# Moving Mamba's and layer 2's weight loads into layer 0, and splitting the starts of layers 1, 2 and 3, in a four-layer conv-attention-Mamba kernel

## The chip, the cores and the metric

The kernel runs on one core of a Trainium2 chip. The engines of a core work side by side, each in the order of its own queue, and wait for one another on semaphores: TensorE (PE in the profile; its weight loads are PEld), VectorE (DVE), ScalarE (ACT), GpSimd (POOL) and SyncE (SP, which here only issues DMA transfers). The metric is the device time of one execution in microseconds (us); lower is better.

## What is computed

The input `x` holds 4 images of 56 x 56 tokens with 128 channels, in float32. Four layers follow one another, each with a residual; constants: 3136 tokens an image, 56 rows.

```
# layer 0: neighbourhood attention, 7 x 7 window, 4 heads, relative bias
x = x + _L0_conv_ref(_gn(x), w_qkv, b_qkv, rpb, w_proj, b_proj)
# layer 1: two Mamba blocks over each row of 56 tokens
x = x + _L1_conv_ref(_gn(x), in_proj_w, conv_w, conv_b, x_proj_w, ...)
t = _to_tokens(x)
# layer 2: additive attention over all earlier tokens, then experts choose 8 tokens each
t = t + _L2_attn_ref(_ln_t(t), W1, b1, w2, b2)
t = t + _L2_ffn_ref(_ln_t(t), gate_w, gate_b, weight1, weight2)
# layer 3: attention over all tokens, then 2 of 8 experts a token
t = t + _L3_attn_ref(_ln_t(t))
t = t + _L3_ffn_ref(_ln_t(t), router_w, router_b, expert_w, expert_b)
```

`_gn` is a group norm over an image (32 groups of 4 channels; mean and variance over all tokens); `_ln_t` a layer norm of each token. A Mamba block multiplies by `in_proj_w`, applies a causal convolution of 4 taps and a silu, makes from that the step `delta` and the vectors B and C, runs `h = exp(delta * A) * h + delta * u * B` along the row, multiplies by C and by a second silu, and projects out. The additive attention of layer 2 scores a pair of tokens by `tanh(f_i + g_j + b1) . w2`.

## The kernel before

All four images stay in SBUF, as `X[b]` of 112 partitions x 28 tiles x 128 channels. A chunk is 4 tiles, 448 tokens, 8 rows; there are 7 an image. The order of PE, ACT, DVE and POOL in each layer is written by hand (`manual_schedule`): what is emitted first stands first in an engine's queue. SP's queue, and instructions outside those regions, are ordered by the framework's scheduler, which may take a transfer that is ready ahead of one that waits. Tiles of a pool are reused; a tile of one buffer (`bufs=1`) is written again only when its readers are done.

**Group norm** (`group_norm_steps`, line 167). For each chunk: four transposes into a PSUM tile (L179), statistics on DVE (`bn_stats`, L190), a copy into the transposed image `xn` on ACT (L191). Then the statistics are aggregated, two small matmuls average over a group (L199), the root is taken on ACT (L213) and polished on DVE, and DVE norms the seven chunks in place (`normed`, L226).

**Layer 0.** `bias_tables` (line 249) reads the constant `toep` in one transfer; `make` forms 7 matmuls (L272) and 7 exponentials (L276) into `tab`, stores that whole into a DRAM table `dtab` (L279) and reads 56 slices of it back into `e_inner` and `e_edge` (L285, L295). On TensorE these matmuls stand ahead of image 0's norm. A unit is one group of key tiles for a chunk: scores (L440), exponentials (L450), multiplication by the tables (L455), weighted sums (L470); `finish` divides (L490) and projects (L496). While image b is worked on, `norm_steps(b + 1)` puts the next image's norm between its units; image 3 has no successor.

**Layer 1.** `layer1_weights` (line 550) issues 20 transfers and forms on DVE the folded weights `in_w` (L604), `A_pick` (L607), `D_diag` (L613) and `xw`; it is called at the layer's start, its pool is opened there. Then image 0's group norm runs to its end (`prepare_image(0)`), and the loop begins. `order` lists 56 blocks (image, chunk, Mamba block) of 16 pairs each. A pair is: decays (L671) and spread inputs (L680) on PE, an exponential on ACT (L696), a product (L701) and a scan (L708) on DVE, a product on POOL (L713). `mamba_pre` spreads the preparation of the next block over the pairs before: the convolution (L826), silu (L838), three projections (L844, L855, L880). All its PSUM passes go through one tile (`m`, pool `l1_m`, one buffer). Steps of a pair are kept in `first` and `last`; the loop starts at pair -18, so that block 0 has its preparation before the first scan. For images 1 to 3 the norm's steps lie among the pairs of the image before. At the end come the last gates (L734, L735), a projection (L752) and the sum into X (L768).

**Layer 2.** `layer2_attention` loads its small weights (W1, b1, w2, place, later, back; 21 transfers), forms `wf` and `wg`, calls `experts2_weights` (11 transfers and a transpose), and then runs `prepare_image(0)` to its end: statistics of 28 tiles (L977, L978), root (L149), 28 norms (L985), 7 transposed chunks (L162), the key part `g` (8 matmuls, L1001) and the queries of the first block (L1027). A block is 7 query tiles (4 blocks an image). Its pieces are `(block, key tile J, quarter q)`: sums on DVE (`adds`, L1042), tangents on ACT (L1051), scores on PE (L1062), then exponentials and weighted sums (L1073, L1076, L1089). With each piece one step is taken from the list `now` or, failing that, from others.

**Layer 3.** `table()` (L1543) asks ScalarE to load the set of tables that has both logarithm and exponential. It is called first, and again after each gelu. `normed_chunk` takes statistics (L1675), a root as `exp(-0.5 ln v)` (L1681, L1682), a Newton step (L1659 to L1662), norms (L1690) and transposes (L1701); image 0's seven chunks run before the first scores (L1597).

Of the kernel before, what the change touches and what calls it, by code (L numbers as in the profile page):

```python
# [2 lines left out]

# [15 lines left out]
S = HW * HW  # L19
# [85 lines left out]
class Hybrid:  # L105
# [37 lines left out]
    def rstd(self, pool, var, shape, eps, tag):  # L143

        nc = self.nc
        ve = self.t(pool, shape, tag + "_ve")
        nc.vector.tensor_scalar(ve, var, eps, None, op0=ALU.add)
        r = self.t(pool, shape, tag + "_r")
        nc.scalar.activation(r, ve, AF.Sqrt)  # L149
        nc.vector.reciprocal(r, r)  # L150
        q = self.t(pool, shape, tag + "_q")
        nc.vector.tensor_mul(q, r, r)
        nc.vector.tensor_mul(q, q, ve)
        nc.vector.tensor_scalar(q, q, -0.5, 1.5, op0=ALU.mult, op1=ALU.add)
        nc.vector.tensor_mul(r, r, q)
        return r
# [10 lines left out]
    def group_norm_steps(self, b, pool, psum, group, pad=0):  # L167


# [3 lines left out]
        got = {}  # L173
        chunk = lambda c: got["xn"][:, c * SEQ : (c + 1) * SEQ, pad:]

        def transposed(c):
            got["ps"] = ps = psum()
            for k in range(TC):
                nc.tensor.transpose(  # L179
                    ps[:, k * TP : (k + 1) * TP], self.X[b][:, TC * c + k, :], self.ident[:TP, :TP]  # L180
                )

        def taken(c):
            if c == 0:
                got["xn"] = self.t(pool, [P, HW, pad + HW], "xnT")
                got["st"] = self.t(pool, [P, NCH, nc.vector.BN_STATS_DIM], "gn_st")
                if pad:
                    nc.gpsimd.memset(got["xn"][:, :, 0:pad], 0.0)
            ps = got["ps"]
            nc.vector.bn_stats(got["st"][:, c, :], ps[:, :CH])  # L190
            nc.scalar.copy(chunk(c), ps[:, :CH].rearrange("p (s t) -> p s t", t=HW))  # L191

        def aggregate():
            got["mv"] = self.t(pool, [P, 2], "gn_mv")
            nc.vector.bn_aggr(got["mv"], got["st"])

        def by_group(of):
            got["ps"] = psum()
            nc.tensor.matmul(got["ps"][:, 0:1], group, of(), start=True, stop=True)  # L199

        def mean():
            got["mean"] = mean = self.t(pool, [P, 1], "gn_mean")
            nc.vector.tensor_copy(mean, got["ps"][:, 0:1])
            got["dev"] = dev = self.t(pool, [P, 1], "gn_dev")
            nc.vector.tensor_sub(dev, got["mv"][:, 0:1], mean)
            nc.vector.tensor_mul(dev, dev, dev)
            nc.vector.tensor_add(dev, dev, got["mv"][:, 1:2])

        def var():
            got["ve"] = ve = self.t(pool, [P, 1], "gn_ve")  # L210
            nc.vector.tensor_scalar(ve, got["ps"][:, 0:1], 1e-5, None, op0=ALU.add)
            got["r"] = self.t(pool, [P, 1], "gn_r")
            nc.scalar.activation(got["r"], ve, AF.Sqrt)  # L213

        def root():
            r, ve = got["r"], got["ve"]
            q = self.t(pool, [P, 1], "gn_q")
            nc.vector.reciprocal(r, r)
            nc.vector.tensor_mul(q, r, r)
            nc.vector.tensor_mul(q, q, ve)  # L220
            nc.vector.tensor_scalar(q, q, -0.5, 1.5, op0=ALU.mult, op1=ALU.add)
            nc.vector.tensor_mul(r, r, q)

        def normed(cs):
            for c in cs:
                nc.vector.tensor_scalar(  # L226
                    chunk(c), chunk(c), got["mean"], got["r"], op0=ALU.subtract, op1=ALU.mult
                )

        bind = lambda f, c: lambda: f(c)  # L230
        return got, (
            [(bind(transposed, c), bind(taken, c)) for c in range(NCH)],
            [
                aggregate, lambda: by_group(lambda: got["mv"][:, 0:1]), mean,
                lambda: by_group(lambda: got["dev"]), var, root,
            ],
            [bind(normed, cs) for cs in (range(0, 2), range(2, 4), range(4, NCH))],
        )

    def group_norm_coarse(self, *args):  # L240

        got, (chunks, stats, norms) = self.group_norm_steps(*args)
        both = lambda fs: lambda: [f() for f in fs]
        return got, [both(fs) for fs in chunks] + [both(stats[:3]), both(stats[3:])] + norms
# [4 lines left out]
    def bias_tables(self, pool, tmp, dr, m):  # L249
# [9 lines left out]
        toep = self.load(tmp, [1 + KR, S], "toep", a["k_toep"])  # L259
# [8 lines left out]
        def make():  # L268
            tab = self.t(tmp, [NH * KR, S], "tab")
            for c in range(NCH):  # L270
                ps = m()[: NH * KR]
                nc.tensor.matmul(  # L272
                    ps[:, :CH], rT.rearrange("p h r -> p (h r)"), toep[:, c * CH : (c + 1) * CH],
                    start=True, stop=True,
                )
                nc.scalar.activation(tab[:, c * CH : (c + 1) * CH], ps[:, :CH], AF.Exp)  # L276

            dtab = dr.tile([NH, KR, HW, HW], F32, name="dtab")
            nc.sync.dma_start(out=dtab.rearrange("h r k j -> (h r) (k j)"), in_=tab)  # L279
# [70 lines left out]
    def layer0(self):  # L350
# [5 lines left out]
        with ExitStack() as ctx:  # L356
# [20 lines left out]
            bproj = self.load(wp, [TP, C], "bproj", a["L0_conv_b_proj"].partition_broadcast(TP))  # L377
            for b in range(1, B):
                self.load_image(b)
            ones = self.t(wp, [TP, HD], "ones")  # L380
# [7 lines left out]
            def norm_steps(b):  # L388
                got, steps = self.group_norm_coarse(b, big, m, group)

                def hand_over():
                    steps[-1]()
                    xn[b] = got["xn"].rearrange("p i j -> p (i j)")

                return steps[:-1] + [hand_over]
# [125 lines left out]
            for k, (b, c) in enumerate(chunks):  # L521
# [9 lines left out]
                if c == 0 and b + 1 < B:  # L531
                    for n, step in enumerate(norm_steps(b + 1)):
                        add(i + 3 * n // 2, step)
            scores(0)
# [15 lines left out]
    def layer1_weights(self, wp):  # L550
        nc, a = self.nc, self.a
        w = {}
# [32 lines left out]
        with ExitStack() as ctx:  # L585
            tmp = ctx.enter_context(self.tc.tile_pool(name="l1_tmp", bufs=1))
            iw = self.load(tmp, [P, NL, DI], "iw", in_w[:, :, 0:DI])
            cw = self.t(tmp, [P, NL, DI, DC], "cw")
            nc.sync.dma_start(
                out=cw.rearrange("p l f k -> p (l f k)"),  # L590
                in_=a["L1_conv_conv_w"].rearrange("l f o k -> (l f o k)").partition_broadcast(P),
            )
            A = self.load(
                tmp, [P, NL, NHALF, DS], "A", by_channel("L1_conv_A_log", "l (h p) n -> p l h n")
            )
            nc.scalar.activation(A, A, AF.Exp)
            xw = self.load(
                tmp, [P, NL, NHALF, DBL], "xw_in", by_channel("L1_conv_x_proj_w", "l (h p) k -> p l h k")
            )
            for at, n, src in ((0, DR, 0), (HD, DR, 0), (2 * HD, DS, DR), (3 * HD, DS, DR + DS)):  # L600
                nc.vector.tensor_copy(w["xw"][:, :, :, at : at + n], xw[:, :, :, src : src + n])
            for l in range(NL):
                for k in range(DC):
# [1221 lines left out]
```

## Time and profile before

| | us |
|---|---|
| median of 3 runs (7923.6 to 7932.92) | 7929.46 |
| the profiled execution | 7930.36 |
| its span, first to last instruction | 7928.6 |
| TensorE busy in the span | 6709.2 (85%) |
| VectorE busy | 6087.8 (77%) |
| ScalarE busy | 5017.8 (63%) |
| GpSimd busy | 2551.3 (32%) |
| mean granted TensorE clock, share of full speed | 0.947 |

The rest of the profile is read stage by stage: each layer has another busiest engine, so the shares over the whole span say little. Three views matter here: the chain of waits (what ended last, followed back), the busy time of each engine in a stretch, and the order of instructions in time. All starts are in us from the start of the span. Three boundaries can be seen in the chain: about 560 (layer 0 to 1), 3544 (1 to 2) and 6407 (2 to 3).

### The profile page before, as it was taken

How to read it: one execution, taken by the hardware profiler on the slowest of the kernel's cores; microseconds unless marked ns; L12 is line 12 of the kernel's file. 1: busy time of each engine (PE TensorE's matmuls, PEld its weight loads, DVE VectorE, ACT ScalarE, POOL GpSimd, SP SyncE). 2: the span in 40 equal slices, each digit the busy share in tenths (PEclk: the TensorE clock that was granted, in tenths of full speed). 3: DMA queues.
4: the chain of work that ended last, by engine and by line, in shares of the span. 5: the costliest groups of instructions: out<-in, count | busy, mean ns of one | idle time of the engine just before them, and what ended most of it. 6: DMA issues, size and time to landing. Idle time of an engine off the chain costs nothing.

```text
span 7928.6 us, 105809 instructions
## 1 busy us (share of the span) xinstructions
PE 6709.2 (85%) x41037; PEld 2666.4 (34%) x41037; DVE 6087.8 (77%) x10253; ACT 5017.8 (63%) x4916; POOL 2551.3 (32%) x1909
## 2 busy tenths in 40 slices
PE   8878988998899899977777777777777889999999
PEld 4442333333333333322222222222222344444544
DVE  6777999999999999986877787887787755344434
ACT  4445555555555555537998899899889964333332
POOL 4545776777777677760000000000001000000000
PEclk9988999999999999988999999999999989999999
DMA  2000000000000000000000000000013101210000
GB/s 54 2 14 1 1 1 1 1 1 1 1 1 1 1 1 1 1 5 1 1 1 1 5 1 1 1 5 1 1 32 114 46 6 43 93 56 6 6 5 6
DMA packets 85490, 102.36 MB, mean 13 GB/s; under 512 B 21158, under 2 KB 50742, under 8 KB 84279
## 3 DMA queue, kind: packets, MB, share of 16 engines
q1 hardware_dynamic: 84985, 95.58, 4.1%
q8 instruction: 322, 5.28, 0.3%
q14 instruction: 183, 1.50, 0.1%
HBM read 85.28 MB, written 10.29 MB: 12 GB/s over the span
## 4 chain that ended last, share of the span: by engine, by line
DVE 35%; PE 32%; ACT 19%; issue 7%; POOL 1%; DVEq 0%; DMA 0%; SPq 0%; ACTq 0%; POOLq 0%
DVE hs L708 19%; ACT th L1051 13%; DVE u L701 7%; PE q L1597 7%; PE o L1608 7%; PE s L1062 6%; DVE th L1042 5%; PE o L1089 3%; PE pe L1762 2%; ACT E L696 2%; PE a L671 1%; ACT L696 1%; PE m L826 1%; DVE e L455 1%; ACT e L1073 1%
## 5 line engine op out<-in xcount | busy, mean ns | idle before, releaser
L1051 ACT ACTIVATE th<-th 128x3136 f32<-128x3136 f32 (+12 forms) x1120 | 2294.6, 2093 | 201.6 <-DVE th L1042 145.1
L1042 DVE TENSOR_SCALAR th<-fT,g 128x784 f32<-128x784 f32 (+6 forms) x3920 | 1918.1, 556 | 490.5 <-PE s L1062 456.4
L713 POOL TENSOR_TENSOR hs<-hs,bc 128x896 f32<-128x896 f32 x896 | 1868.2, 2085 | 798.8 <-DVE hs L708 772.7
L1062 PE MATMUL s<-th,place 128*32 128x392 f32 (+7 forms) x14336 | 1489.3, 493 | 671.2 <-ACT th L1051 668.3
L708 DVE TENSOR_TENSOR_SCAN hs<-E,u 128x896 f32<-128x896 f32 x896 | 1810.0, 2020 | 115.8 <-DVE u L701 2.0
L696 ACT ACTIVATE E<-a 128x896 f32<-128x896 f32 x896 | 821.5, 917 | 805.9 <-PE u L680 332.7
L671 PE MATMUL a<-delta,A_pick 32*128 32x448 f32 x3584 | 983.6, 601 | 154.5 <-ACT E L696 147.1
L680 PE MATMUL u<-du,pick 32*128 32x448 f32 x3584 | 980.9, 603 | 46.5 <-DVE hs L708 46.4
L701 DVE TENSOR_TENSOR u<-u,bc 128x896 f32<-128x896 f32 x896 | 963.8, 1076 | 48.0 <-PE u L680 47.9
L1062 PEld LDWEIGHTS s<-th,place 128*32 128x32 f32 (+1 forms) x14336 | 426.5, 111 | 1616.7 <-ACT th L1051 1083.9
L1602 ACT ACTIVATE e<-q,shift 128x448 f32<-128x448 f32 (+1 forms) x700 | 440.7, 633 | 730.9 <-PE q L1597 730.4
L1080 POOL TENSOR_TENSOR e<-e,later 112x112 f32<-112x112 f32 x112 | 80.4, 718 | 2318.0 <-ACT e L1073 1677.3
L1608 PE MATMUL o<-e,xk 128*128 128x448 f32 (+1 forms) x1400 | 653.6, 549 | 25.7 <-ACT oT L1583 25.7
L1767 DVE SCALAR_TENSOR_TENSOR X<-pe,r_gate,X 112x128 f32<-112x128 f32 x896 | 314.1, 351 | 454.4 <-PE pe L1762 418.9
L1597 PE MATMUL q<-xT 128*128 128x448 f32 (+1 forms) x1400 | 654.1, 549 | 6.0 <-ACT e L1602 5.9
L671 PEld LDWEIGHTS a<-delta,A_pick 32*128 32x128 f32 x3584 | 296.5, 188 | 699.1 <-ACT E L696 468.5
L719 PE MATMUL y<-hs,sum 128*32 128x448 f32 x3584 | 441.4, 563 | 4.4 <-POOL hs L713 4.4
L1089 PE MATMUL o<-e,xa 112*128 112x392 f32 (+5 forms) x1024 | 426.3, 539 | 1.1 <-POOL e L1080 1.1
L680 PEld LDWEIGHTS u<-du,pick 32*128 32x128 f32 x3584 | 297.8, 189 | 214.4 <-DVE hs L708 196.9
L1608 PEld LDWEIGHTS o<-e,xk 128*128 128x128 f32 (+1 forms) x1400 | 262.0, 191 | 309.9 <-issue 275.0
L1597 PEld LDWEIGHTS q<-xT 128*128 128x128 f32 (+1 forms) x1400 | 248.7, 189 | 243.6 <-issue 211.8
L1696 POOL MEMSET lc_xa<- 112x4 f32 x28 | 3.1, 110 | 893.2 <-DVE lc_xa L1690 555.6
(251 smaller groups left out, 7197.7 us busy)
## 6 DMA issues: line engine op xcount, KB each, us to landing
wide<-in_L_ffn_weight SPq DMA_DIRECT2D x64, 1024.0 KB
X<-in_x SPq DMA_DIRECT2D x8, 784.0 KB
out<-X SPq DMA_DIRECT2D x28, 224.0 KB
M<-wide SPq DMA_DIRECT2D x4, 784.0 KB
wide<-M SPq DMA_DIRECT2D x4, 784.0 KB
e_edge<-dtab SPq DMA_DIRECT2D x42, 49.0 KB
cw<-in_L_conv_conv_w SPq DMA_DIRECT2D x1, 1024.0 KB
c_h<-in_L_ffn_weight SPq DMA_DIRECT2D x16, 64.0 KB
```

The costliest lines, as they stand in the source:

```text
L671: nc.tensor.matmul(halves(to)[:, k], w["A"][own, order[j][2], f, q, :], pre[j]["delta"][own, f], start=True, stop=True,)
L680: nc.tensor.matmul(halves(to)[:, k], w["pick"][own, q, :], pre[j]["du"][own, f], start=True, stop=True,)
L696: nc.scalar.activation(E[p + 1], t, AF.Exp)
L701: nc.vector.tensor_mul(v, v, pre[p // PAIRS]["bc"][:, 0:1].to_broadcast([P, 2, CH]))
L708: nc.vector.tensor_tensor_scan(flat, E.pop(p), V.pop(p), 0.0, op0=ALU.mult, op1=ALU.add)
L713: nc.gpsimd.tensor_mul(HS[p], HS[p], bc[:, 1:2].to_broadcast([P, 2, CH]))
L1042: nc.vector.tensor_scalar(th[i][:, blk, lo:hi], fT[j][:, lo:hi], im[order[j][0]]["g"][:, at : at + 1], None, op0=ALU.add,)
L1051: nc.scalar.activation(own, own, AF.Tanh)
L1062: nc.tensor.matmul(ps[j, J][QW * blk : QW * blk + rows, h, lo:hi], place[:, off : off + rows], z[:, blk, h * HALF + lo : h * HALF + hi], s ...
L1089: nc.tensor.matmul(po[j][:, h, lo:hi], im[b]["xa"][:, J, :], e[:, h * HALF + lo : h * HALF + hi], start=(J == 0), stop=(J == t + ((h + 1) ...
L1597: nc.tensor.matmul(ps[:n, :CH], xT[b][:, k : k + n], xT[b][:, c * CH : (c + 1) * CH], start=True, stop=True,)
L1608: nc.tensor.matmul(po[b, c], xk[b][:n, t, :], es.pop((b, c, t))[:n], start=(t == 0), stop=(t == N - 1))
```

## The change

- `layer1_weights` is called within layer 0, after the tables and ahead of the loads of images 1 to 3; its pool is opened ahead of layer 0. Its transfers are the same, except that the taps `cw` come in four pieces through one buffer. What it computes is returned as a list of 41 steps, and layer 0 runs one at every second unit from unit `first[2]` on.
- `toep` is read and `tab` stored in seven pieces of a chunk, with two buffers each.
- While image 3 is worked on in layer 0, `next_norm` takes image 0's statistics for layer 1 (transposes, `bn_stats`, group part; no copy, no norm).
- Layer 1 begins with image 0's chunk 0 turned again and scaled on ACT straight out of PSUM (`scaled`: `Identity` with `bias=-mean*r`, `scale=r`); the other six chunks follow at pairs -5, -4 and -3. For images 1 to 3 DVE's norm is replaced by `scaled` on ACT, one chunk a pair.
- Layer 2's small weights are loaded in layer 0, behind the images (`layer2_loads`). Image 0's statistics for layer 2 run at the end of layer 1 (20 tiles right after the last scan, 8 tiles and the root after the last sum into X).
- Layer 2 begins with 8 tiles: two chunks normed and turned, keys for 112 of 392 groups, the first queries. The other five chunks, the remaining keys, the second block's queries and `experts2_weights` are steps in `now`. `wg` is cleared on POOL instead of DVE.
- In layer 3 `table` stands twice among the first steps, at 1 and 3, instead of ahead of them.
- Some tiles of the root in layer 2 have one buffer instead of two.

```diff
         def make():
-            tab = self.t(tmp, [NH * KR, S], "tab")
+            flat = dtab.rearrange("h r k j -> (h r) (k j)")
             for c in range(NCH):
+                own = slice(c * CH, (c + 1) * CH)
+                toep = self.t(tmp, [1 + KR, CH], "toep", bufs=2)
+                nc.sync.dma_start(out=toep, in_=a["k_toep"][:, own])
+                tab = self.t(tmp, [NH * KR, CH], "tab", bufs=2)
...
+                nc.scalar.activation(tab, ps[:, :CH], AF.Exp)
+                nc.sync.dma_start(out=flat[:, own], in_=tab)
...
             bproj = self.load(wp, [TP, C], "bproj", a["L0_conv_b_proj"].partition_broadcast(TP))
+            tmp = ctx.enter_context(tc.tile_pool(name="l1_tmp", bufs=1))
+            next_weights = self.layer1_weights(wp1, tmp)
             for b in range(1, B):
                 self.load_image(b)
+            self.layer2_loads()
...
+            def next_norm():
+                g = self.first_norm = self.group_norm(0, wp1, group)
+                parts = g.groups(m)
+                both = lambda fs: lambda: [f() for f in fs]
+                chunk = lambda c: lambda: (g.turn(c, m), g.stats(c))
+                return [chunk(c) for c in range(NCH)] + [both(parts[:3]), both(parts[3:])]
...
-                if c == 0 and b + 1 < B:
-                    for n, step in enumerate(norm_steps(b + 1)):
+                if c == 0:
+                    for n, step in enumerate(norm_steps(b + 1) if b + 1 < B else next_norm()):
                         add(i + 3 * n // 2, step)
+            for n, step in enumerate(next_weights):
+                add(first[2] + 2 * n, step)
...
+        def scaled(c, of=None):
+            of = g.chunk(c) if of is None else by_row(of[:, :CH])
+            nc.scalar.activation(g.chunk(c), of, AF.Identity, bias=g.off, scale=g.r)
...
+        def projection(i, k):
+            l, f = divmod(i, NHALF)
+            own = slice(f * P, (f + 1) * P)
+            nc.vector.tensor_mul(w["in"][:, l, k, own], iw[:, l, own], cw[i][:, :, k])
+            if k == DC - 1 and i + 1 < NL * NHALF:
+                load_taps(i + 1)
...
+                        add(last, at - 2 * PAIRS + 3 + c, g.scaled, c)
...
-            chunks, stats, norms = prepare_image(0)
-            for step in [f for fs in chunks for f in fs] + stats + norms:
-                step()
+            g = self.first_norm
+            g.place(big, DC - 1)
+            hand_over(0, g)
+            for c in range(NCH):
+                turned = lambda c=c: (g.turn(c, m), g.scaled(c, g.ps))
+                if c == 0:
+                    turned()
+                else:
+                    add(last, -PAIRS + 11 + (c - 1) // 2, turned)
+            for n, step in enumerate(self.first_stats()):
+                add(first if n < 20 else last, n_pairs if n < 20 else n_pairs + 10, step)
...
+                if b == 0:
+
+                    here, end = 2, 2 * CH // JG
+                    chunk = lambda c: [bind(norm, TC * c), bind(norm, TC * c + 2), bind(turn, c)]
+                    start = [f for c in range(here) for f in chunk(c)]
+                    start += [bind(ones, 0, TC * here)] + key_steps(0, end)
+                    rest = [f for c in range(here, NCH) for f in chunk(c)]
+                    rest[-1] = lambda: (turn(NCH - 1), ones(TC * here, NT))
+                    return start, rest + key_steps(end, S // JG)
...
+            nc.gpsimd.memset(wg, 0.0)
+            start, now = prepare_image(0)
+            for step in start[:7]:
+                step()
+            nc.vector.tensor_copy(wf, W1[:, 0:1, :].to_broadcast([P, JG, AH]))
+            for j in range(JG):
+                nc.vector.tensor_copy(wg[:, j, j * AH : (j + 1) * AH], W1[:, 1, :])
+            nc.vector.tensor_scalar(place, place, w2, None, op0=ALU.mult)
+            for step in start[7:]:
                 step()
             queries(0)
-            now, later_on, behind, held = [], [], [], False
+            now.append(lambda: queries(1))
+            later_on, behind, held = [], [], False
...
+            weights2 = lambda: setattr(self, "w2", self.experts2_weights(self.f2_w, m))
+            assert len(now) < first[1] - 1
+            now.append(weights2)
...
-            table()
             at = {}
-            start = [(k + 2 * c, step) for c in range(NCH) for k, step in prepare_chunk(0, c)]
+            start = [(1, table), (3, table)]
+            start += [(k + 2 * c, step) for c in range(NCH) for k, step in prepare_chunk(0, c)]
...
-    k.layer0()
-    k.layer1()
+    with ExitStack() as ctx1:
+        wp = ctx1.enter_context(tc.tile_pool(name="l1_w", bufs=1))
+        k.layer0(wp)
+        k.layer1()
```

## The prediction

> **What bounds it now.** I read the page's chain of waits first, then the busy time by stretch, then the chain in each stretch that the change touches. By the landmarks of the chain layer 0 runs to 560 us, layer 1 to 3544, layer 2 to 6407, layer 3 to the end. Inside the layers one engine is nearly full (VectorE in layer 1, ScalarE in 2, TensorE in 3); between them it is not:
>
> ```profile
> 560.00:600.00 40.00, 7.20 (x28) 4.98 (x28) 16.54 (x54) 5.49 (x10) 0.27 (x1) 0.50 0.21 61
> ...
> 3544.00:3555.00 11.00, 0.00 (x0) 0.00 (x0) 2.01 (x11) 0.00 (x0) 0.00 (x0) 0.50 0.12 18
> 3555.00:3605.00 50.00, 20.73 (x49) 9.63 (x49) 25.44 (x103) 4.55 (x7) 0.15 (x1) 0.60 0.05 13
> 3605.00:3662.00 57.00, 40.26 (x332) 13.64 (x332) 40.79 (x105) 47.02 (x38) 2.72 (x6) 0.83 0.00 1
> ```
>
> The columns are stretch, length, busy PE, weight load, VectorE, ScalarE, GpSimd, then granted clock and DMA. The two gaps, 40 and 61 us, hold almost nothing of what their layer is made of. The chain says what fills them:
>
> ```profile
> 568.04 5.31 DMA cw<-in_L_conv_conv_w
> ...
> 600.57 6.20 PE m L826 x8
> ...
> 630.66 1.79 PE a L671 x4
> ...
> 1284.55 3.01 DVE xnT L226 x3
> ...
> 3570.12 7.27 DVE xa L985 x28
> ...
> 3588.06 11.62 PE h L1001 x16
> ...
> 3604.84 2.83 ACT th L1051
> ```
>
> Start and length in us. The first gap is loads, then weight preparation, then image 0's statistics, until the first convolution (L826). The second is loads, statistics, norm, seven transposed chunks and the keys (L1001), until the first tangent.
>
> **Entry of layer 1.** Now the first convolution starts at 600.57. After the change only a transpose (1.01, row of L179 in this gap) and a ScalarE scaling (0.63, as L834, same tile with a bias) stand between TensorE's last projection (ends 559.8) and it; with two handovers of 0.1 it starts at 561.6: -39. The other six chunks are turned at steps -5 to -3, through one PSUM tile, so each waits for the copy of the one before: 1.01 + 0.63 + 0.15 = 1.8, six are 11. TensorE is in order and behind them queue the first decays (L671 at 630.66), which follow their predecessors without a gap, and behind those the first scan: +11, at least 8 should the transposes run at the 0.55 they take in layer 0. Sum -28 (-31 to -26).
>
> **What that puts into layer 0.** *Work.* Image 0's statistics: 7 x 0.62 on VectorE (L190), 28 transposes, and the group part with its square root. In the trace a chunk of layer 0 takes 15.9 us undisturbed and 22.2 with the present norm steps, but there ScalarE's copies wait for VectorE, and those are absent here. VectorE's own time, 7 x 0.62 + 2, is 6.3, two table loads 2.6; I take 11 (5 to 16). Weight preparation: 16 rates x 0.21, 16 projections at half of 0.54, 8 small ones, 9 us of VectorE in 41 steps; VectorE is 86% busy at 400-500 us, so the waits for ScalarE hide about half: +4, 9 without that cover.
>
> *Queues.* The trace of SP:
>
> ```profile
> 0.74 0.45 SPq L132 DMA_DIRECT2D toep<-in_k_toep  x1
> ...
> 2.91 1.24 SPq L126 DMA_DIRECT2D X<-in_x  x2
> ...
> 4.20 3.06 SPq L132 DMA_DIRECT2D group<-in_k_group  x1
> ...
> 16.70 0.33 SPq L279 DMA_DIRECT2D dtab<-tab  x1
> ...
> 21.92 10.51 SPq L285 DMA_DIRECT2D e_edge<-dtab  x21
> ...
> 49.83 7.40 SPq L126 DMA_DIRECT2D X<-in_x  x4
> ```
>
> Start, issue time, transfer. The first bias multiply starts at 39.84, released by the last e_inner transfer: the tables bound the start. Now `toep` is read first; afterwards its first piece stands behind image 0 (1.57 MB at the 179 GB/s of the first 20 us: 2.9 + 8.8, landing near 13.5), so the table matmuls start 8 us later than now (5.43). Pieces share two buffers, so piece c+2 is issued after matmul c: with the 2.6 us from the issue of rpbT to its use and 1.5 us a matmul pair the seven end 3.4 later than now. TensorE has them ahead of image 0's transposes, so the norm is late by as much. Twenty Mamba loads (1.5 MB in all) queue between those round trips; by 179 GB/s they could add 8, I take 4. Third, image 1 now comes behind 56 edge loads (0.49 each) and those twenty: if all go first, its first half lands near 74 where TensorE, late by 15, asks at 58 (43.18 now): 16 of stall; none if it is issued while the tables are made, as the trace shows it for that half (9.33, ahead of the table's store). Nearer to the latter: 5. The 21 loads of layer 2 come after all images. Sum +20; bounds +3 (only the round trips) and +46 (8 + 3 + 8 + 16, and 11 for image 1's second half and images behind it).
>
> On splitting, the Trainium skill, DMA: Bandwidth & Descriptors (Rules for kernel authors), speaks against this change: coalesce, since a transfer under 64 KB is mostly fixed cost, some 2.0 us each. An estimate from that page for the three extra round trips is 3 x 2.0 = 6 us instead of 3.4, a total 3 us slower.
>
> **Layer 1's body.** For images 1 to 3 seven VectorE norms go to ScalarE. In the chain they are runs of 2, 2 and 3 of 1.0 us on the engine that sets the layer, 7 us an image: -21. ScalarE gets 7 x 0.65, one per pair; it is busy 1581 of 2862 us (672 to 3534), but a late exponential then costs a little: -19 (-21 to -13).
>
> **Entry of layer 2.** From the last X add (ends 3543.95) to the first tangent are 60.9 us. Afterwards: 8 statistics x 0.40 (28 take 11.1) = 3.2, root 3.1 (3567.04 to 3570.12), four norms 1.0, two transposes with copies 3.4, the spread weights 1.2 (L917, L924, L929), keys 112/392 of 11.62 = 3.3, bias 0.3, queries 2.9, four adds 2.3: 20.7. So -40. The other twenty statistics, 7.9 us, lie in VectorE's 9.18 us of idle before that X add; without that cover they would cost 7.9. The loads' 10 us of issue disappear from here.
>
> What is left out (20 norms, 5.2; five chunks turned, 5 x 1.01 plus copies; keys 280/392 of 11.62 = 8.3; queries and expert weights) runs one step a piece in the first block, 3605 to 3662. ScalarE sets that block (47 of 57) and gets only 1.3 more; TensorE has 17 free and gets 13.4, but the keys fall into its last short pieces, and the second block's queries behind them. From 1.3 (all hidden) to 20 (TensorE's 13.4 and VectorE's 7 in the open); nearest is TensorE's own sum: +13. Together -27 (-39 to -20).
>
> **Layer 3.**
>
> ```profile
> 6409.64 1.28 ACT L1681 ACT_TABLE_LOAD   x1 [12.19 <-DVE lc_mv L1676]
> 6410.94 0.30 ACT L1681 ACTIVATE lc_r<-lc_mv,eps 112x4 f32<-112x4 f32 x1
> ```
>
> And on the page, with its idle time and releaser last:
>
> ```profile
> L1597 PE MATMUL q<-xT 128*128 128x448 f32 (+1 forms) x1400 | 654.1, 549 | 6.0 <-ACT e L1602 5.9
> ```
>
> Eighteen roots reload two sets each. The set of L1543 is loaded at 0.73 us, at the kernel's head: as the first ScalarE instruction of its region it drifted up. Of the new pair the first may drift again; the second stands behind a root, stays, and saves the rest. At entry VectorE works without a gap from 6416.59 to 6439, so six shorter roots (2.57 each) gain only its other gaps: -2 (0 to -6). Then 12 roots delay TensorE: q starts every 1.50 us, but 2.29 apart at 6459.45 and 6461.74. 12 x 0.79 = 9.5; the row above has 5.9 in all: -7 (-10 to -4).
>
> The Trainium skill, ScalarE: Activation LUTs (What ACT_TABLE_LOAD costs), adds a drain of 1.38 us to each load of 1.28. The trace disagrees: Ln starts 0.02 us after the load ends, and the load of 6458.05 stands 0.02 after the exponential before it. By the page these 24 loads would free 33 us more of ScalarE; I go by the trace.
>
> **Sum.** +20 +11 +4 -28 -19 -27 -2 -7 = **-48 us** on the span of 7928.6. Its execution took 7930.4, the median is 7929.5; from the median: **7881**.
>
> **Rivals.**
> *Late tables.* Every round trip waits behind weights, image 1 behind all edges (+46), and statistics and preparation find no cover (16 and 9): +71 instead of +35: 7917. For it: the queue's DMA share is 0.80 in the first 20 us. Against: image 1 slipped ahead before.
> *Both table loads drift.* Then layer 3 keeps its 36 loads: 7890. For it: L1543 at 0.73. Against: the gelu's copy (6972.96) stayed in place.
> *More overlap.* The six late chunks, the preparation and half of the block's extra work hide: -11 -4 -7 -20 (start near its lower end): 7840. Against: in-order TensorE.
> *Slower.* One mechanism: SP's issue in layer 0 blocks. `group` took 3.06 instead of 0.45 to issue, behind image 0. If the 20 weight loads and 14 table pieces each cost 2.6 more, 88 us come ahead of image 1 instead of the 12 that I have for them: 7957. It decides above 2.2 us for each of these 34 (64 + 12 over 34). Against: the next five issues took 0.43 to 0.57.
>
> **Chances.** This kernel's runs tell 0.2%, 16 us, from no change. Forecast 0.62, more overlap 0.08, drifting loads 0.08: faster 0.78. Late tables 0.14: within 0.2%. Slower 0.08. Range: from -90, where the good ends of two or three terms meet, to 7920, past the late tables: 7840 to 7920.
>
> **What would show it.** First bias multiply near 55 instead of 39.84, no TensorE gap over 5 us at image 1; layer 0 ends near 595; first convolution 2 us after it; no L226 in layer 1 past image 0; first tangent about 20 us after layer 1's last X add and the next block some 70 after that; 4 to 6 table loads at L1681, L1682 and the preload. I am wrong if layer 0 grows by over 60, or if the first block of layer 2 takes over 80.

## The result and the profile after

| | before | after |
|---|---|---|
| median, us | 7931.19 (7923.6 to 7937.37, 4 runs) | 7882.52 (7877.41 to 7889.87, 4 runs) |
| span of the profiled execution | 7928.6 | 7883.1 |
| ratio of the times | | 0.9935, 95% interval 0.9924 to 0.9947 |

48.7 us by the medians and 45.5 by the two spans, where 48 were forecast, and the time lies 1.5 us from the 7881. Line numbers have moved: the conv is L889 now, the first decays L723, the transposes of a chunk L184, the keys of layer 2 L1085, the tangents L1149, layer 3's q L1707, its roots L1791 and L1792.

The busy times by stretch, in the columns of the prediction's first fence. The stretches are the entry of layer 2 and its first block:

```profile
3541.10:3559.50 18.40, 7.58 (x28) 5.53 (x28) 11.57 (x50) 2.04 (x3) 0.49 (x2) 0.72 0.13 37
3559.50:3622.20 62.70, 50.37 (x369) 17.57 (x369) 45.66 (x126) 45.78 (x39) 3.61 (x7) 0.89 0.00 1
```

The 61 us ahead of layer 2's first tangent are 18.4, and the first block has grown to 62.7 (TensorE busy for 50 of them). The chain of waits (start, length) shows both entries:

```profile
602.22 1.21 PE m L529 x4
604.41 5.12 PE m L889 x8
...
632.54 1.02 PE m L184 x4
...
642.68 1.79 PE a L723 x4
...
3550.62 3.74 PE h L1085 x16
```

The convolution (L889) follows layer 0's last projection (L529) at once; the 40 us between them are gone. Ahead of the decays (L723) now stand the six late chunks, 1.83 us apart from 632.54 on. The keys that the first tangent waits for take 3.74 instead of 11.62.

What layer 0 paid stands in the order of time (start, length, idle time before it and what ended it):

```profile
24.34 1.75 PE L184 MATMUL m<-ident,X 112*128 112x112 f32 x8
...
26.88 9.56 SPq L295 DMA_DIRECT2D e_edge<-dtab  x21
...
43.32 9.61 SPq L295 DMA_DIRECT2D e_edge<-dtab  x21
...
48.27 0.68 DVE L488 TENSOR_TENSOR e<-e,e_edge 112x504 f32<-112x504 f32 x1 [3.20 <-ACT e L483]
...
55.48 8.42 SPq L127 DMA_DIRECT2D X<-in_x  x3
...
65.65 0.98 PE L184 MATMUL m<-ident,X 112*128 112x112 f32 x4 [13.89 <-DMA X<-in_x]
...
0.73 1.28 ACT L1653 ACT_TABLE_LOAD   x1 [0.73 <-PEq L1924]
...
6376.19 1.28 ACT L1653 ACT_TABLE_LOAD   x1
6377.48 0.30 ACT L1791 ACTIVATE lc_r<-lc_mv,eps 112x4 f32<-112x4 f32 x1
```

The table's pieces run from 26.88 to 52.93 (42 edges, and 14 inner ones between the two rows). Image 1 was issued behind all of them and five weights, at 55.48, and TensorE stood 13.89 us for it: the largest single loss of the change. The Toeplitz matmuls began at 11.82 instead of 5.43, so that image 0's transposes behind them begin at 24.34 instead of 16.03, and the first multiplication by the tables (L488) at 48.27 instead of 39.84; its wait ends with an exponential on ScalarE, no longer with a table piece. Of layer 3's two table loads (L1653) one drifted to the kernel's head, the other stayed at 6376.19, and from there the roots need no load. The page's row for q says what that is worth to TensorE (6.0 us of idle time before):

```profile
L1707 PE MATMUL q<-xT 128*128 128x448 f32 (+1 forms) x1400 | 654.7, 550 | 2.3 <-ACT e L1712 2.2
```

From landmark to landmark the 45.5 us come together so: first chunk's sum into X (L519) 63.95 to 87.61, +23.7; the rest of layer 0 up to its last projection +20.0; from there to the first convolution -39.8; first decay behind it (30.0 to 38.2) +8.2; first decay to last scan (2903.5 to 2888.7) -14.8; last sum into X to first tangent (60.9 to 18.4) -42.5; first block (55.0 to 62.7) +7.7; the rest of layer 2 up to its last tangent -1.3; from there to layer 3's first exponential (its entry) -1.2; its rest -5.5.

### The profile page after: what moved, and what is told of

It reads as the page before. It is cut to its first block, busy times and chain, and to the rows that moved or that the text cites. A ratio compares the mean times of both kernels' runs of the same rounds, so it can differ in the third digit from the quotient of the medians.

```text
span 7883.1 us, 105890 instructions
## 1 busy us (share of the span) xinstructions
PE 6718.3 (85%) x41081; PEld 2672.6 (34%) x41081; DVE 6070.7 (77%) x10241; ACT 4990.0 (63%) x4903; POOL 2552.6 (32%) x1911
## 4 chain that ended last, share of the span: by engine, by line
PE 35%; DVE 33%; ACT 20%; issue 7%; POOL 1%; DVEq 0%; DMA 0%; ACTq 0%; SPq 0%; POOLq 0%
DVE hs L760 17%; ACT th L1149 13%; PE q L1707 7%; PE o L1718 7%; DVE u L753 6%; PE s L1160 6%; DVE th L1140 4%; PE o L1187 2%; PE pe L1872 2%; ACT E L748 2%; PE a L723 2%; PE m L889 2%; DVE e L488 1%; ACT L748 1%; PE y L771 1%
## 5 line engine op out<-in xcount | busy, mean ns | idle before, releaser
L1149 ACT ACTIVATE th<-th 128x3136 f32<-128x3136 f32 (+12 forms) x1120 | 2293.6, 2093 | 194.6 <-DVE th L1140 138.4
L723 PE MATMUL a<-delta,A_pick 32*128 32x448 f32 x3584 | 983.2, 601 | 148.0 <-ACT E L748 140.4
L1707 PE MATMUL q<-xT 128*128 128x448 f32 (+1 forms) x1400 | 654.7, 550 | 2.3 <-ACT e L1712 2.2
L723 PEld LDWEIGHTS a<-delta,A_pick 32*128 32x128 f32 x3584 | 295.7, 188 | 697.4 <-ACT E L748 466.5
L1707 PEld LDWEIGHTS q<-xT 128*128 128x128 f32 (+1 forms) x1400 | 249.0, 189 | 238.1 <-issue 213.0
```

The source lines that it names most:

```text
L723: nc.tensor.matmul(halves(to)[:, k], w["A"][own, order[j][2], f, q, :], pre[j]["delta"][own, f], start=True, stop=True,)
L1149: nc.scalar.activation(own, own, AF.Tanh)
L1707: nc.tensor.matmul(ps[:n, :CH], xT[b][:, k : k + n], xT[b][:, c * CH : (c + 1) * CH], start=True, stop=True,)
```

## Experiments

Each kernel is the changed one with one thing undone, moved or done alone. The profiled spans stand against 7883.1, the medians against 7882.52.

| label | what differs | span, us | median, us | ratio to before, 95% interval |
|---|---|---|---|---|
| u1_dve_norm | norm of images 1 to 3 on VectorE | 7902.2 | 7905.10 | 0.9954 (0.9939 to 0.9969) |
| u2_table_ahead | one table load, ahead of layer 3's steps | 7890.0 | 7893.28 | 0.9942 (0.9925 to 0.9959) |
| u3_image1_first | image 1 ahead of the weights | 7871.7 | 7871.42 | 0.9912 (0.9897 to 0.9927) |
| u4_weights_in_l1 | weights at layer 1's start | 7892.4 | 7893.19 | 0.9944 (0.9929 to 0.9959) |
| w1_stats_in_l1 | image 0's statistics at layer 1's start | 7886.9 | 7891.00 | 0.9944 (0.9929 to 0.9958) |
| u5_whole_start | layer 2 begun with 28 tiles | 7899.6 | 7901.25 | 0.9955 (0.9939 to 0.9971) |
| v1_toep_first | first two Toeplitz pieces first | 7885.8 | 7888.27 | 0.9939 (0.9920 to 0.9958) |
| v3_late_hidden | late chunks between the steps | 7875.6 | 7877.73 | 0.9924 (0.9907 to 0.9940) |
| w2_image1_gated | image 1 between the edges | 7871.2 | 7872.33 | 0.9920 (0.9903 to 0.9936) |
| w3_gated_hidden | w2 and v3 | 7864.2 | 7867.69 | 0.9914 (0.9899 to 0.9928) |
| v4_all | u3, v1 and v3 | 7856.1 | 7859.40 | 0.9902 (0.9886 to 0.9917) |

Whole spans tell less than they seem to. Chunks 0 to 27 of layer 0 took 494.6 to 500.9 us in kernels in which nothing of that stretch was changed (u1, u2, u5 and v3 beside the changed kernel); layer 2 from its second block to its last tangent took 2735 to 2748, layer 3 from its first exponential 1475 to 1483 (u2 aside). A difference under some 8 us is therefore read at the place of the edit, and the span is only a check.

### The weights' loads and preparation

```diff
-            tmp = ctx.enter_context(tc.tile_pool(name="l1_tmp", bufs=1))
-            next_weights = self.layer1_weights(wp1, tmp)
+            self.wp1 = wp1
...
-            for n, step in enumerate(next_weights):
-                add(first[2] + 2 * n, step)
...
+            with tc.tile_pool(name="l1_tmp", bufs=1) as tmp:
+                for step in self.layer1_weights(self.wp1, tmp):
+                    step()
             w = self.w1
```

> The changed kernel, with the Mamba weights loaded and formed at the start of layer 1 again; the statistics taken ahead, the chunked table and all else stay. Theory: in layer 0 this frees the 13.9 us wait for image 1, some 8 us of weight preparation on VectorE, and 2 to 5 us of the table's round trips, together 24 to 27; at the entry of layer 1 the loads and the preparation come back into the open, 18 to 22 us. So moving the weights as it was done was worth nothing: the span is 7874 to 7883. Rival: the preparation is hidden in layer 0 and the wait for image 1 stays without the weights; then the entry's 20 us are lost nearly whole, and the span is 7895 or more.

7892.4: the theory fell, and the rival doesn't hold either, for the wait for image 1 is gone. In the order of time of this kernel:

```profile
594.44 15.55 SPq L631 DMA_DIRECT2D cw<-in_L_conv_conv_w  x4
...
612.68 1.26 DVE L641 TENSOR_TENSOR in_w<-iw,cw 128x128 f32<-128x128 f32 x4 [3.05 <-DMA cw<-in_L_conv_conv_w]
...
614.86 1.83 PE L889 MATMUL m<-xnT,in_w 128*128 128x448 f32 x2 [22.06 <-ACT xnT L247]
```

The four pieces of the taps go through one buffer, so each is loaded only when the one before is used up, 4.3 to 4.6 us apart, the last projection weights are formed at 612.68, and TensorE stands 22.06 us (0.99 in the changed kernel). Layer 0's last projection ends 10.6 us earlier (592.8 for 603.4): 4.7 of it are there at the first chunk (82.91 for 87.61): image 1 is issued early (10.80 and 16.46) and nothing waits for it, but the loads of images 1 to 3 now stand between the pieces of the tables, the edges begin at 37.70 and the first multiply slips to 58.88. Another 5.2 come up to chunk 20, where kernels with the same code differ by 4.1 (385.7 to 389.8 us from the first chunk's sum; here 384.4). The weights in layer 0 are worth 21.1 - 10.6 = 10.5 us in these two profiles, and at most 16 if only the first 4.7 count.

### Image 0's statistics

```diff
-                    for n, step in enumerate(norm_steps(b + 1) if b + 1 < B else next_norm()):
+                    for n, step in enumerate(norm_steps(b + 1) if b + 1 < B else []):
...
-            g = self.first_norm
+            g = self.group_norm(0, big, w["group"])
             g.place(big, DC - 1)
+            for c in range(NCH):
+                g.turn(c, m)
+                g.stats(c)
+                g.raw(c)
+            for step in g.groups(m):
+                step()
             hand_over(0, g)
             for c in range(NCH):
-                turned = lambda c=c: (g.turn(c, m), g.scaled(c, g.ps))
...
+                g.scaled(c)
```

> Image 0's statistics for layer 1 are taken at layer 1's start again (all seven chunks turned, measured and kept raw, then scaled on ScalarE), while the Mamba weights stay in layer 0; layer 0 has nothing in its last image for layer 1. Theory (the two preparations lay side by side in the kernel before, with the statistics the longer, so the one without the other brings next to nothing): layer 0 ends about 11 us earlier (last image), the first convolution stands 36 to 42 us behind the last projection (1 us now, 22 with only the weights put back), the six late chunks are gone from the first chunk's end (about 8 us), so the first decay is 17 to 22 us later and the span 7898 to 7908. Rival (the two are additive: of the 39.8 us the weights were 21 and the statistics 19): first convolution 17 to 20 us behind the projection, span 7878 to 7886.

A miss again, and the rival is right to within a microsecond (7886.9): the convolution stands 20.6 us behind the last projection. The chain of this kernel:

```profile
592.46 0.69 DVE X L532
593.15 0.55 DVE gn_st L194
...
612.94 6.20 PE m L891 x8
```

and the order of time of the kernel before, which would have said so:

```profile
579.60 1.72 DVE L607 SCALAR_TENSOR_TENSOR A_pick<-pick,A 128x128 f32<-128x128 f32 x8
581.35 0.63 DVE L190 BATCH_NORM_STATS2 gn_st<-m 128x6 f32<-128x448 f32 x1
```

The first statistics stood behind the last weight on VectorE's queue: the 39.8 us were 21 of weights and 19 of statistics, one after the other. What the statistics gain at the entry they lose elsewhere: chunks 20 to 27 take 99.5 us here and 111.1 with them (+11.7), and the late chunks cost 8.2 (from the convolution to the first decay 30.0 here, 38.2 with them). 19.6 - 11.7 - 8.2 is nothing, and the first decay starts at 642.96 against 642.61. This part of the change brought nothing.

### The late chunks

```diff
-                turned = lambda c=c: (g.turn(c, m), g.scaled(c, g.ps))
+                turned = lambda c=c: (g.turn(c, (lambda: self.t(ps_u, [P, 1024], "u")) if c else m), g.scaled(c, g.ps))
...
-                    add(last, -PAIRS + 11 + (c - 1) // 2, turned)
+                    add(last, -PAIRS + (0, 2, 2, 5, 7, 9, 10)[c], turned)
```

> The six late chunks of image 0 are turned between the steps of layer 1's first chunk, through the PSUM tiles of the scan's inputs, not one after the other behind it. Theory: now they are a chain of six times 1.83 us (632.54 to 643.45) in which TensorE and ScalarE wait for each other; spread out they cost at most ScalarE's 6 x 0.73 = 4.4 us: first decay 6.6 to 11 us earlier, span 7872 to 7877. Rival (ScalarE's queue is the bound of the first chunk, so the copies push its silu and softplus back by as much as the chain gave): span 7881 to 7885.

The span is the theory's, the mechanism only half. From the convolution to the first decay are 34.1 us instead of 38.2, so 4.1 are won; layer 0, in which nothing differs, happened to be 6.5 faster. In w3_gated_hidden and v4_all the same stretch takes 32.5 and 32.4, so the edit is worth 4 to 6. From the chain of w3_gated_hidden (start, length):

```profile
613.96 0.73 ACT xnT L247
614.68 0.43 ACT bc L932
```

A late chunk's copy of 0.73 us lies on ScalarE ahead of the copy `bc` that the next projection waits for. Spread out, the late chunks are still in the chain, with less waiting around them.

### Image 1 and the tables on one queue

```diff
+            self.load_image(1)
             next_weights = self.layer1_weights(wp1, tmp)
-            for b in range(1, B):
+            for b in range(2, B):
```

> The changed kernel, with image 1's load ahead of the Mamba weights. Theory: TensorE's wait of 13.9 us for image 1 (at 51.8 us) comes only from the order in SP's queue; it goes, and the first multiplication by the tables (48.3) moves by less than 4; the end of layer 0 comes 10 to 14 us earlier, the span is 7869 to 7873. Rival: the 1.6 MB then stand ahead of the table's pieces and edges, and what is won at image 1 is lost at the first multiplication (later by 8 or more); the span stays within 4 us.

The span (7871.7) and the end of layer 0 (11.4 earlier) are the theory's, but one of its two conditions failed: image 1's wait is gone, but its transfer (issued at 11.25 and 17.02) now runs ahead of the later Toeplitz pieces, and the first bias multiply slips from 48.27 to 55.21, by 6.9 and not by less than 4. The first chunk's sum is 8.7 earlier (78.89); the other 2.7 of layer 0 lie within its scatter.

```diff
+        for c in range(2):
+            fetch(c)
         rT = self.t(tmp, [1 + KR, NH, KR], "rpbT")
...
-                toep = self.t(tmp, [1 + KR, CH], "toep", bufs=2)
-                nc.sync.dma_start(out=toep, in_=a["k_toep"][:, own])
+                toep = pieces.pop(c)
...
+                fetch(c + 2)
                 nc.scalar.activation(tab, ps[:, :CH], AF.Exp)
```

> The first two Toeplitz pieces of the bias tables are loaded ahead of image 0 and of the bias table's own loads; the later ones follow through the same two buffers. Theory: the Toeplitz matmuls stand behind the image on the load queue (11.82 us against 5.43 before); with them first, table, edges and image 1 all move up together: first Toeplitz matmul at 5 to 7 us, first bias multiply at 42 to 45 (48.27 now), end of layer 0 and span 4 to 7 us earlier: 7876 to 7879. Rival (image 1 is bound by the volume of the loads ahead of it, so the wait for image 1 grows by what the start saves): span 7881 to 7885.

The theory fell: 7885.8, and the first chunk's sum at 87.54. In the order of time of v1_toep_first:

```profile
13.40 3.19 PE L292 MATMUL m<-toep,rpbT 14*52 14x448 f32 x4 [5.22 <-DMA toep<-in_k_toep]
```

The first matmuls start at 4.99, but the next pieces stand behind image 0 all the same, and TensorE waits 5.22 us for them; the edges begin 0.9 us earlier, and image 1's first transpose stays at 65.79. So the load queue was to be reordered where image 1 stands:

```diff
                         nc.sync.dma_start(
                             out=inner[own, :, 1 + k, :],
...
+                for t in (0, NT // 2):
+                    nc.gpsimd.tensor_copy(self.X[1][:HW, t, 0:1], edge[0][:HW, 3, 0, NB - 1, 0:1])
+                self.load_image(1)
```

> Image 1 is loaded between the tables' inner part and the second set of 21 edges, held there by a copy of one element out of the last first-set edge, so that it neither stands behind all 56 table pieces and the weights nor runs ahead of the tables. Theory (what counts is the place on the one in-order load queue): first bias multiply unmoved at 48 to 49, image 1's load issued near 43 and its first transposition at 53 to 56 (65.65 now, 56.96 with it ahead of the tables) with a wait of at most 3 us, first chunk's X add at 74 to 78 (87.61 now, 78.89 with it ahead), span 7866 to 7873. Rival (image 1 shares its bandwidth with the table pieces still in flight and lands no earlier than 60): X add at 80 to 84, span 7875 to 7880.

```profile
43.73 1.14 SPq L127 DMA_DIRECT2D X<-in_x  x2
44.93 14.99 SPq L295 DMA_DIRECT2D e_edge<-dtab  x21
...
54.17 0.95 PE L184 MATMUL m<-ident,X 112*128 112x112 f32 x4
```

Confirmed: TensorE no longer waits, the first chunk's sum is at 74.82, 12.8 us earlier than in the changed kernel, and the convolution 15.3 earlier. The first multiply is 2.5 later than there (50.78), which was not expected; but it starts at 50.99 in u1_dve_norm, where nothing of the start differs, so this edit is not shown to move it.

### VectorE's norm in layer 1

```diff
-                        add(last, at - 2 * PAIRS + 3 + c, g.scaled, c)
...
+                    for k, cs in enumerate((range(0, 2), range(2, 4), range(4, NCH))):
+                        add(last, at - 2 * PAIRS + 3 + 2 * k, g.normed, cs)
```

> The changed kernel, with the norm of images 1 to 3 in layer 1 on VectorE again. Theory: of the 45 us that the span lost, 15 came from these 21 instructions leaving VectorE (the stretch from the first steady scan to the last scan's end shrank by 14.7 us); so that stretch grows by 13 to 21 us, the rest stays, and the span is 7896 to 7904. Rival: layer 1 shrank for another reason (the first scans, the clock); then this kernel's stretch stays within 3 us of the changed one's.

Confirmed in kind: the span is 7902.2, and from first decay to last scan are 2901.2 us, against 2888.7 in the changed kernel and 2879 to 2889 in the ten others. The 12.5 lie just under the theory's 13 to 21; the rest of the span's 19.1 lies elsewhere. VectorE's instructions in the order of time of this kernel, and GpSimd's:

```profile
1276.95 2.68 DVE L241 TENSOR_SCALAR xnT<-xnT,gn_mean,gn_r 128x448 f32<-128x448 f32 x2
...
1294.74 3.10 DVE L241 TENSOR_SCALAR xnT<-xnT,gn_mean,gn_r 128x448 f32<-128x448 f32 x3
...
1277.18 2.20 POOL L765 TENSOR_TENSOR hs<-hs,bc 128x896 f32<-128x896 f32 x1 [1.05 <-DVE hs L760]
```

Two norms right behind a scan take 2.68 us and three 3.10, though one takes 0.50 in layer 0; see the last section. In the chain of the kernel before, a run of two is as long:

```profile
1266.76 2.60 DVE xnT L226 x2
```

### The start of layer 2 and the tables of layer 3

```diff
-                    here, end = 2, 2 * CH // JG
+                    here, end = NCH, S // JG
...
-                    rest[-1] = lambda: (turn(NCH - 1), ones(TC * here, NT))
-                    return start, rest + key_steps(end, S // JG)
+                    return start, []
...
-            for step in start[:7]:
+            for step in start[:-9]:
...
-            for step in start[7:]:
+            for step in start[-9:]:
```

> Layer 2 begins with all 28 tiles (7 chunks) of keys, ones and statistics, as in the kernel before, and the first block carries none of it; nothing else differs from the changed kernel (span 7883.1 us). Theory (the prediction's): the part moves work from a stretch where every engine waits for the previous step into a block whose engines are partly idle, so undoing it makes the first tangent start 17 to 23 us later after layer 1's last X add (18.4 us now), and gives back the 6.4 us that the first blocks now lose: span 7894 to 7900. Rival (the work is only moved: each microsecond saved at the entry is paid again in the first block): span 7881 to 7886. A second rival, the table load being what counted and not the tiles: also 7881 to 7886, with the entry no longer.

The busy times by stretch, entry and first block of this kernel:

```profile
3534.90:3570.70 35.80, 21.65 (x50) 9.70 (x50) 18.80 (x72) 3.10 (x5) 0.48 (x2) 0.69 0.07 19
3570.70:3623.70 53.00, 37.56 (x331) 13.16 (x331) 38.92 (x102) 45.12 (x38) 2.66 (x6) 0.87 0.00 1
```

Entry 17.4 us longer, block 9.7 shorter: from the last sum into X to the second block are 88.8 us, against 81.1 with 8 tiles and 115.9 before. So the theory holds at the entry, but the block gives back 9.7 and not 6.4: the split is worth 7.7 us, and the loads and statistics moved ahead 27.1. The span's 16.5 says more than that; the rest lies in stretches that the edit doesn't touch (12.1 in layer 2 behind the first block), so that it fell into the theory's range is chance.

```diff
-            start = [(1, table), (3, table)]
-            start += [(k + 2 * c, step) for c in range(NCH) for k, step in prepare_chunk(0, c)]
+            table()
+            start = [(k + 2 * c, step) for c in range(NCH) for k, step in prepare_chunk(0, c)]
```

> The changed kernel, with one preload of the table set ahead of layer 3's first steps, as before. Theory: the preload drifts to the kernel's head, 36 loads return at the two root lines, the steady part of layer 3 grows by 5 to 7 us and its entry by 1 to 2. Rival: the loads lie beside TensorE's work; then they return and the time stays within 2 us.

Confirmed. In the order of time of this kernel every root loads both sets:

```profile
6374.49 1.28 ACT L1791 ACT_TABLE_LOAD   x1 [15.26 <-DVE lc_mv L1786]
...
6376.10 1.28 ACT L1792 ACT_TABLE_LOAD   x1
...
6377.62 1.28 ACT L1791 ACT_TABLE_LOAD   x1
```

36 loads in the roots are back, TensorE's idle time ahead of q is 6.0 us again, the entry of layer 3 is 1.2 longer and its rest 5.1.

### The pieces together

v4_all has the edits of u3, v1 and v3, w3_gated_hidden those of w2 and v3.

> Image 1 loaded ahead of the weights (span 7871.7 alone), the first two Toeplitz pieces ahead of image 0, and the late chunks turned between the steps of the first chunk. Theory: the three mend different waits (the load queue's order twice, and a chain on two engines), and with image 1 no longer behind the edges the Toeplitz pieces are worth the 7 to 11 us by which the tables come late there (first bias multiply at 55.21): span 7871.7 - 7 to 11 - 6 to 11 = 7850 to 7859. Rival (image 1 ahead of the tables takes the bandwidth that the Toeplitz pieces need, so the two are worth no more than one): 7861 to 7867.

> Image 1 between the inner part and the second edges, and the six late chunks turned between the first chunk's steps. Theory: the landmarks of the two alone add up: X add of the first chunk at 74 to 78, first decay 32 to 35 us behind the first convolution (38.2 now, 34.1 with the late chunks spread alone); span 7860 to 7869, at least 14 us under the changed kernel. Rival (spread late chunks were worth nothing and that kernel's gain was the scatter of layer 0): the decay still 32 to 35 us behind the convolution, but the first scan's gain lost by the last scan, span 7868 to 7875.

Both spans lie where their theories had them: 7856.1 and 7864.2, and w3_gated_hidden has its landmarks too (sum at 74.79, decay 32.5 behind the convolution). In v4_all the Toeplitz pieces, worth nothing alone, bring the first multiply from 55.21 back to 49.62: they count only where image 1 goes ahead of the tables. But that is 5.6 where 7 to 11 were expected, and the late chunks give 5.8 where 6 to 11 were: at the first decay this kernel is 10.6 us ahead of u3_image1_first, not 13 to 22, so the span's 15.6 is theirs only in part. The first decays start at 620.68 and 621.54 (642.61 in the changed kernel), so the two orders are the same thing at that point, and the 8 us between the spans come from layer 2 and later. By the medians they are 23 and 15 us faster than the changed kernel. The ratios are 0.9902 and 0.9914 against its 0.9935; only v4_all's interval lies clear of that one (0.9917 at most, against 0.9924 at least).

## Why the prediction was right

The mechanism was right everywhere but at layer 0's start. That the sum came within 2.5 us of the spans' 45.5 is partly luck: layer 0 cost 8.6 more than forecast and layer 2's entry and first block together gained 7.8 more, and the smaller errors nearly cancel as well.

- **Layer 0's start, +20; measured +23.7.** Two errors of opposite sign. The first bias multiply was to slip to 55; it slipped to 48.27. Of the 15 only 8.4 came: the Toeplitz matmuls start 6.4 later (forecast 8), their pieces add 1.9 (3.4), and the weights between them nothing that can be seen (4). Image 0's transposes stand behind these matmuls and slip by the same 8.3, and the tables, which the prediction took for the bound, are there before the multiply's other input. The third item, 5 us of stall at image 1, is the step that failed: 13.89, the upper half of its 0 to 16. The trace of before showed half of image 1 issued early; with the weights in program order ahead of it none was, and the 56 pieces at 0.46 to 0.48 us each stood ahead of it.
- **Preparation, +4; measured 1 to 5** (u4 against the kernels with the same code). **Statistics, +11; measured 11.7** (w1). The rest of layer 0 grew by 20.0 and not by 15; 2.8 us up to chunk 20 are there without the weights too and were not tried.
- **Layer 1's entry, -39 and +11; measured -39.8 and +8.2.** The late chunks cost 10.7 with the wait before them, as forecast, but the convolution and the first projection ahead of them take 5.12 and 1.78 instead of 6.20 and 3.25 (granted clock 0.65 and 1.00 in these stretches, 0.54 and 0.66 before), so that 2.6 come back. The prediction names the two preparations in the 39 one after the other, but did not weigh each by itself: the weights net 10.5 to 16, the statistics nothing.
- **Layer 1's body, -19; measured -14.8**, and -15 to -24 in the ten other kernels with the norm on ScalarE. Right in kind and, with this scatter, in size. The price was misread, though: the chain has 2.60 for two norms and not 2.0, and in images 1 and 2 one run of two is not on it, so that its 19.4 us are near the 21 by chance.
- **Layer 2's entry, -40; measured -42.5. First block, +13; measured +7.7.** The mis-sized term. TensorE is busy 50.4 us there, 10 more than in the 57 us of before, and part of that lies in its former gaps; the forecast took all of its left-over work, 13, as the price. The rival of more overlap, with 7 of the 13 hidden, was nearer there.
- **Layer 3, -2 and -7; measured -1.2 and -5.5**, one load drifted and the other stayed.
- **The rivals.** SP's issue did not block: table pieces and weights took 0.30 to 0.51 us each to issue, `group` at the start (2.06) aside; only the images' loads behind the edges (six in 19.67) and layer 2's W1 (3.71) took longer. Nor were the tables late: the first multiply ended its wait with ScalarE's exponential. The further overlap of the late chunks is real but 4 to 6 us, not 11.

## What to carry to other kernels

When a preparation is moved ahead into a full stage, weigh each part by what it frees where it was and what it costs where it goes: here loads with little work of their own were worth it, statistics with work on the same engines were not. A transfer that is moved into an in-order queue is also priced by what stands behind it (image 1's place: 12.8 us at the first chunk). For effects below the scatter of the whole run read the distance between two landmarks on either side of the edit, and don't count the difference of spans as its proof.

## What the hardware showed beside

VectorE's norm is 0.50 us in layer 0, but in layer 1 the second one behind a scan takes up to 2.27: it starts while GpSimd's product of 2.2 us, released by the same scan, runs (1277.18 to 1279.38), and ends 0.25 behind it. The view of that line in u1_dve_norm (least, median and greatest ns, first and last start):

```profile
L241 DVE TENSOR_SCALAR xnT<-xnT,gn_mean,gn_r x49: 487/502/2273, 37.4 to 2752.1; 128x448 f32<-128x448 f32 x49
```

and rows of its order of time, the second norm of layer 1 and, in layer 0, three norms beside a multiplication on GpSimd:

```profile
1277.36 2.27 DVE L241 TENSOR_SCALAR xnT<-xnT,gn_mean,gn_r 128x448 f32<-128x448 f32 x1
...
151.96 1.35 DVE L241 TENSOR_SCALAR xnT<-xnT,gn_mean,gn_r 128x448 f32<-128x448 f32 x3
...
151.81 1.66 POOL L488 TENSOR_TENSOR e<-e,e_inner 112x56 f32<-112x56 f32 x1
```

There the norms keep their 0.50 and GpSimd is the slow one: its multiplication takes 1.66 where the median of its size is 0.39, and ends 0.16 behind the last norm.

So seven norms of an image in layer 1 cost 2.68 + 2.67 + 3.10 = 8.45 us and not 3.5. The Trainium skill, SBUF — State Buffer (SBUF: two separate sides), says that VectorE in its two-port mode and GpSimd share one pair of ports, that whichever starts first holds it for a whole instruction, and that the other blocks. The lengths above agree with it, on either side; no run here told it from another cause.
